# A two-layer graph network with experts on one core: the first six tiles of layer 1 begun in a branch beside layer 0's last blocks, and the last outputs added by pairs of tiles

## The chip, the core and the metric

The kernel runs on one core of a Trainium2 chip. A core has five engines, each with its own queue of instructions in a fixed order: PE (TensorE, matrix products), DVE (VectorE), ACT (ScalarE), POOL (GpSimd) and SP (SyncE, here only a sender of transfers). Transfers between the chip's memory (DRAM) and the core's on-chip memory are carried out by DMA engines, which all queues share. The metric is the device time of one execution in microseconds (us); the time of a kernel is the median of its runs.

## The reference, cut to what matters

```python
# layer 0
x = x + relu(adj @ (layernorm(x) @ W) + b)
x = x + moe(layernorm(x))        # 8 experts, the two best per row, hidden size 1024, relu
# layer 1
x = x + relu(top700(tanh(adj * adj) where adj > 0) @ (tanh(layernorm(x) @ W_proj + b_proj) @ W_gcn) + b_gcn)
x = x + moe2(layernorm(x))       # 8 experts, the two best per row, hidden size 256, gelu, plus its input
```

There are 3327 rows of 256 numbers in float32, and adj is 3327 x 3327, with about nine entries per row that are not zero. In both mixtures of experts each row goes to the two experts with the best scores, and the two results are added to it with weights.

## The kernel before, in words

Rows lie in 26 tiles of 128. `x` and `s` are on chip for all tiles: `x` holds the rows, `s` the features that the graph step multiplies by adj. Six large buffers, `ring[0]` to `ring[5]`, hold pieces of adj, weights of experts, or expert outputs that are read back, one after another.

Each layer goes through these stages:

1. *Features.* Every tile is normalized (`statistics` at L244 makes mean and inverse deviation, with two DVE instructions a tile and then twelve small ones for the whole group; `layernorm` at L266 writes `xn`), turned by PE (`by_features`, L278), and multiplied by one or two weight matrices (L288, L1019), which gives `s`.
2. *Aggregation* (`aggregate`, L321). For 13 panels of 256 columns of adj, PE forms the product with `s` (L335), and DVE adds bias, relu and x. After each panel the rows are normalized, scored and written to a list per expert in DRAM, `xlist`, by indirect transfers from POOL (L459).
3. *Expert blocks* (`experts`, L683). A block is up to 256 rows of one expert ("pair", 128 rows are a "single"). Its `step` (L830) has SP load list rows and weights of a later block into the ring (L734 to L756), PE turns rows (L767) and multiplies twice (L778 with ACT's function at L785, then L811), DVE adds the bias and scales (L818, L819), and POOL scatters the result rows to `ys` in DRAM (L459). The first eight blocks of a layer (EARLY) are planned from the first 18 tiles (`plan_early`), while the aggregation still runs; `plan` places the others. With these inputs layer 0 runs 30 blocks, numbered 0 to 29. Blocks 28 and 29 are pairs, 27 is a single. A branch (`rest`, L848) holds four spare singles, which are skipped here.
4. *Seam or end.* Both result rows of each row are read back from `ys` into the ring (`load_outputs`, L873, on SP's queue) and added to `x` by two DVE instructions (`add_loaded`, L884). Between the layers this is the head of layer 1's features: `turned_pairs` (L1001) goes through groups of tiles, first one of two, then six of four (FOURS, L82), alternating between `ring[5]` and `ring[4]`: read, add, statistics, normalize, turn. A read waits for all scatters of layer 0 (`follow`). At the end of the kernel `finish` (L1130) does read, add and output.

Layer 1's end already has a branch (L1136): if the first 14 tiles are complete after the early blocks, their results are read, added and written between the last blocks; the tiles from 14 on follow in `finish`. In the other arm all tiles follow. `covered` (L621) makes the flag on DVE, from the number of rows that the first tiles send to each expert and the number of rows that the early blocks do.

What sets the order: the program is written in the order of the source, and a planner of the compiler sorts the instructions of each stretch without branches onto the engines' queues, by its own model of when they are ready, the earlier in the source first; all waits are inserted by it. `issue_after` (in `behind`, L202) puts the instructions of a block behind a given one on that one's engine. It adds no wait between engines. Instructions inside a branch are not mixed with those outside. `declare_no_dep` and the groups next to it say which transfers need not wait for one another.

Of the kernel before, what the change touches and what calls it, by code (L numbers as in the profile page):

```python
# [10 lines left out]
F32 = mybir.dt.float32  # L11
BF16 = mybir.dt.bfloat16
I32 = mybir.dt.int32
AF = mybir.ActivationFunctionType
# [8 lines left out]
P = 128  # L23
# [53 lines left out]

FIRST_TILES = 14
FREE_PAN = NPAN - RING // NCHUNK
# [6 lines left out]
def gnn_moe_two_layers(  # L86
# [91 lines left out]

    ids_i = const.tile([P, NT, K], I32, name="ids_i")
    nc.gpsimd.iota(ids_i, pattern=[[K * P, NT], [1, K]], base=0, channel_multiplier=K)  # L180
    ids = const.tile([P, NT, K], F32, name="ids")
    nc.vector.tensor_copy(ids, ids_i)

    spare_i = const.tile([P, LATE, SG], I32, name="spare_i")
    nc.gpsimd.iota(spare_i, pattern=[[SB, LATE], [P, SG]], base=SPARE, channel_multiplier=1)
# [57 lines left out]

    def statistics(t0, n):  # L244


        st = work.tile([P, n, 6], F32, name="ln_st")
        mv = work.tile([P, n, 2], F32, name="ln_mv")
        for g in range(n):
            nc.vector.bn_stats(out=st[:, g, :], in_=x[:, t0 + g, :])  # L250
            nc.vector.bn_aggr(out=mv[:, g, :], in_=st[:, g, :])
        ve = work.tile([P, n], F32, name="ln_ve")
        nc.vector.tensor_scalar(ve, mv[:, :, 1], EPS, None, ALU.add)  # L253
        half = work.tile([P, n], I32, name="ln_half")
        nc.vector.tensor_scalar(half, ve.bitcast(I32), 1, None, ALU.logical_shift_right)
        guess = work.tile([P, n], I32, name="ln_guess")
        nc.vector.tensor_scalar(guess, half, -1.0, float(0x5F3759DF), ALU.mult, ALU.add)
        rs = guess.bitcast(F32)
        nw = work.tile([P, n], F32, name="ln_nw")
        for _ in range(3):  # L260
            nc.vector.scalar_tensor_tensor(nw, rs, -0.5, rs, ALU.mult, ALU.mult)  # L261
            nc.vector.tensor_tensor(nw, nw, ve, ALU.mult)  # L262
            nc.vector.scalar_tensor_tensor(rs, nw, 1.5, rs, ALU.add, ALU.mult)  # L263
        return mv, rs

    def layernorm(t0, n, stats=None, at=0):  # L266


        mv, rs = stats or statistics(t0, n)
        xn = work.tile([P, n, K, RW], F32, name="xn")  # L270
        for g in range(n):
            last_normalized[:] = [nc.vector.tensor_scalar(  # L272
                xn[:, g, 0, 0:D], x[:, t0 + g, :], mv[:, at + g, 0:1], rs[:, at + g : at + g + 1],
                ALU.subtract, ALU.mult,
            )]
        return xn
# [652 lines left out]
    def count(pan, chunks):  # L929
# [9 lines left out]
    layer0 = experts(  # L939
        p0, 3, xlist0, ys0, "0", FIXED[0], H, AF.Relu, f0_w1T, f0_b1, f0_w2T, f0_b2,  # L940
        nc.vector.tensor_copy,
# [49 lines left out]
    late = plan()  # L991
    layer0.rest(late, number_of_singles(late))
    rows_written.clear()

    first_pool.close()
# [5 lines left out]
    def turned_pairs():  # L1001


        for i, (t0, n0) in enumerate(FOURS):

            yt = ring[RING - 1 - i % NCHUNK][:, 0 : n0 * K * D]
            yt = yt.rearrange("p (n d) -> p n d", n=n0)
            with ExitStack() as queue:
                if normal:
                    queue.enter_context(tc.issue_after(normal[-1].ins))  # L1010
                add_outputs(yt, ys0, t0, n0)
                stats = statistics(t0, n0)
                for at in range(0, n0, 2):
                    xnT = by_features(layernorm(t0 + at, 2, stats, at), 2)
                    if at + 2 == n0:
                        normal.append(last_normalized[0])
                    yield t0 + at, xnT
# [118 lines left out]
    with tc.If(complete > 0) as arms:  # L1136
# [18 lines left out]
        layer1.rest(late, n_singles)  # L1155
        finish([(t, n) for t, n in FOURS if t >= FIRST_TILES])
    with arms.Else():
# [144 lines left out]
```

## Time and profile before

| what | value |
|---|---|
| median of 3 runs | 1272.45 us (1272.04 to 1273.16) |
| the profiled execution, its own time | 1283.92 us |
| its span, from the first to the last instruction | 1282.1 us |
| PE busy | 1208.2 us, 94% of the span |
| DVE, ACT, POOL busy | 713.0 (56%), 519.5 (41%), 286.3 us (22%) |
| chain: PE's aggregation, L335 | 23% of the span |
| chain: DVE's adding of expert outputs, L887 | 1% of the span |
| last scatter of layer 0 | sent at 747.40 us |
| last scatter of layer 1 | sent at 1260.45 us |

The profile page gives busy times by engine, then the chain of work that ended last, followed back from the last instruction, then groups of instructions by source line. The trace behind it answers closer questions: a timeline of single instructions, in which a bracket tells how long the engine was idle before and who released it, and tables of windows. A busy PE is not a PE at its peak, since its instructions overlap. In rows such as `L887 TENSOR_TENSOR x<-x,ring` the line is that of the source, and `out<-in` are the names of the tiles.

### The profile page before, as it was taken

The numbers are of one execution on the slowest core, as the hardware profiler recorded it, in microseconds if no ns is written. First come the engines' busy times: TensorE is split into PE (matmuls) and PEld (weight loads), VectorE is DVE, ScalarE is ACT, GpSimd is POOL, SyncE is SP. The second block draws the span as 40 slices with busy tenths as digits, with TensorE's granted clock in tenths as the row PEclk, the third lists the DMA queues.
The fourth block names the chain that finished last, engine by engine and source line by source line (L and its number), as shares of the span: only waits on it lengthen the run. The fifth ranks groups of instructions, "written<-read, shape, count | busy, mean of one in ns | idle before, by whom it ended". The sixth has DMA issues, their size and how long they took to land. (4 is left out here: it accounts for less than half of the span.)

```text
span 1282.1 us, 18560 instructions
## 1 busy us (share of the span) xinstructions
PE 1208.2 (94%) x5815; PEld 1036.9 (81%) x5815; DVE 713.0 (56%) x2918; ACT 519.5 (41%) x963; POOL 286.3 (22%) x364
## 2 busy tenths in 40 slices
PE   5999999999999999999999959999999999989991
PEld 4888888888888888888888847788888888867771
DVE  8167677676761111111111149579989998574453
ACT  3797545550122222322222215985554551133330
POOL 2132131221321111111111100203123131354432
PEclk9999999999999999999999979999999999999996
DMA  9676454453167566666666357145544452547785
GB/s 362 161 253 207 169 194 177 176 180 122 59 236 234 185 213 200 218 205 210 211 207 209 110 209 281 60 156 193 177 168 169 161 188 75 185 138 212 210 270 192
DMA packets 119458, 241.70 MB, mean 189 GB/s; under 512 B 21472, under 2 KB 89840, under 8 KB 112304
## 3 DMA queue, kind: packets, MB, share of 16 engines
q1 hardware_dynamic: 106576, 206.91, 48.7%
q0 software_dynamic: 11184, 31.85, 6.8%
q10 hardware_dynamic: 1584, 1.57, 0.4%
q8 instruction: 52, 0.85, 0.3%
q14 instruction: 62, 0.51, 0.1%
HBM read 203.99 MB, written 36.33 MB: 187 GB/s over the span
## 5 line engine op out<-in xcount | busy, mean ns | idle before, releaser
L335 PE MATMUL ps_g<-s,ring 128*128 128x256 f32 x2704 | 588.3, 380 | 1.6 <-issue 1.6
L335 PEld LDWEIGHTS ps_g<-s,ring 128*128 128x128 f32 x2704 | 511.9, 190 | 70.5 <-issue 1.7
L785 ACT ACTIVATE hT<-ps_h,ring 128x256 f32<-128x256 f32 (+1 forms) x304 | 139.1, 459 | 369.5 <-PE ps_h L778 322.1
L778 PE MATMUL ps_h<-xT,ring 128*128 128x256 f32 (+1 forms) x1208 | 259.9, 368 | 4.0 <-ACT xT L770 2.1
L778 PEld LDWEIGHTS ps_h<-xT,ring 128*128 128x128 f32 x1208 | 212.0, 191 | 43.4 <-ACT hT L785 4.8
L811 PE MATMUL ps_y<-ring,hT 128*128 128x256 f32 x928 | 208.7, 380 | 0.0
L355 DVE SCALAR_TENSOR_TENSOR rt_product<-xn,gate 128x256 f32<-128x256 f32 x400 | 197.6, 494 | 12.5
L459 POOL DMA_INDIRECT ys<-y,index x114 | 111.8, 981 | 408.2 <-DVE y L819 278.5
L811 PEld LDWEIGHTS ps_y<-ring,hT 128*128 128x128 f32 x928 | 173.5, 191 | 21.9
L459 POOL DMA_INDIRECT xlist<-xn,rt_idx x104 | 105.7, 1016 | 378.9 <-DVE ln_ve L253 288.4
L934 ACT ACTIVATE sign<-ring,below 128x416 bf16<-128x416 f32 x208 | 133.5, 642 | 74.4 <-DMA ring<-in_adjT 51.7
L818 DVE TENSOR_TENSOR y<-ps_y,ring 128x256 f32<-128x256 f32 x64 | 27.1, 424 | 154.8 <-PE ps_y L811 154.8
L770 DVE COPY xT<-ptb 128x512 f32<-128x512 f32 (+1 forms) x30 | 19.7, 655 | 161.5 <-PE ptb L767 161.5
L1046 ACT ACTIVATE ring<-ring 128x3328 f32<-128x3328 f32 x22 | 65.5, 2977 | 91.4 <-DVE ring L1045 57.8
L300 DVE TENSOR_TENSOR gnn_t<-ps_g,gnn_b_sb 128x256 f32<-128x256 f32 x52 | 22.0, 423 | 116.1 <-PE ps_g L335 116.0
L1047 ACT ACTIVATE ring<-ring 128x3328 f32<-128x3328 f32 x22 | 65.5, 2978 | 0.7
L811 PE MATMUL ps_y<-s,hT 128*128 x200 | 51.2, 395 | 10.8 <-issue 4.8
L811 PEld LDWEIGHTS ps_y<-s,hT 128*128 128x128 f32 x200 | 35.6, 191 | 20.4 <-issue 10.6
L420 ACT ACTIVATE rt_d<-rt_d 128x2 f32<-128x2 f32 x26 | 5.3, 202 | 114.1 <-DVE rt_d L419 114.1
L887 DVE TENSOR_TENSOR x<-x,ring 128x1024 f32<-128x1024 f32 (+1 forms) x34 | 33.0, 972 | 30.0 <-DMA ring<-ys 29.7
L250 DVE BATCH_NORM_STATS2 ln_st<-x 128x6 f32<-128x256 f32 x104 | 42.8, 420 | 4.8 <-DMA x<-in_x 3.7
L819 DVE TENSOR_SCALAR y<-y,ring 128x256 f32<-128x256 f32 x114 | 42.1, 371 | 3.6 <-DVEq L850 0.3
(171 smaller groups left out, 906.1 us busy)
## 6 DMA issues: line engine op xcount, KB each, us to landing
ring<-in_adjT SPq DMA_DIRECT2D x52, 1664.0 KB
ring<-in_f_w1T SPq DMA_DIRECT2D x30, 1024.0 KB
ring<-in_f_w2T SPq DMA_DIRECT2D x30, 1024.0 KB
ring<-xlist SPq DMA_DIRECT2D x52, 258.0 KB
ring<-ys SPq DMA_DIRECT2D x9, 1024.0 KB
ring<-in_f_w SPq DMA_DIRECT2D x36, 256.0 KB
ring<-in_f_b SPq DMA_DIRECT2D x34, 128.0 KB
xlist<-hT SPq DMA_DIRECT2D x16, 258.0 KB
```

The costliest lines, as they stand in the source:

```text
L250: nc.vector.bn_stats(out=st[:, g, :], in_=x[:, t0 + g, :])
L335: nc.tensor.matmul(ps[it], lhsT=chunks[k][:, c, ts(it, P)], rhs=s[:, j, :], start=(j == 0), stop=(j == NT - 1),)
L355: nc.vector.scalar_tensor_tensor(product, xn[:, g, 0, 0:D], 1.0, gate[:, e, :], ALU.mult, ALU.mult, accum_out=sc[:, g, e : e + 1],)
L459: d = nc.gpsimd.indirect_dma_start(out=a[:, :], out_offset=bass.IndirectOffsetOnAxis(ap=index, axis=0), in_=rows_, in_offset=None,)
L778: nc.tensor.matmul(ps, lhsT=w1[:, c, ts(hc, P)], rhs=xT[:, c, :], start=(c == 0), stop=(c == DC - 1),)
L785: nc.scalar.activation(hT[:, hc, :], ps, func, bias=bb1[:, hc : hc + 1])
L811: last_product[:] = [nc.tensor.matmul(ps, lhsT=hT[:, hc, ts(g, P)], rhs=w2[:, hc, :], start=(hc == 0), stop=(hc == hc_n - 1),)]
L819: last_y[:] = [nc.vector.tensor_scalar(y[:, g, :], y[:, g, :], xb[:, g, WT : WT + 1], None, ALU.mult)]
L887: nc.vector.tensor_tensor(x_t, x_t, yt[:, :, k * D : (k + 1) * D], ALU.add)
L934: nc.scalar.activation(sign, a[:, :, ts(i, GROUP)], AF.Sign, bias=below, accum_out=positive[:, pan, i, k : k + 1],)
L1046: nc.scalar.activation(a, a, AF.Square)
L1047: nc.scalar.activation(a, a, AF.Tanh)
```

## The change

Six tiles (BEGUN) are begun inside layer 0. After block 26 a flag is read: are all rows of the first six tiles done by the early blocks? If so, the last three blocks run in an arm that has more in it: after block 27 SP reads the outputs of tiles 0 and 1 and of tiles 2 to 5 into `s`, which is free then, and after block 28 DVE adds them to `x`, makes the statistics of all six tiles (kept in `begun_stats`) and normalizes tiles 0 and 1 (kept in `begun_xn`). If not, the other arm runs the same blocks and does this work after them. In `turned_pairs` the first group then has only the turning left, and the second group its normalizing; the first read of the seam is that of tiles 6 to 9. To make room, two integer tables share one buffer, and layer 0's `y` and `index` have two buffers instead of three. At the end, in the complete arm, tiles 14 to 25 are read, added and written by twos instead of by fours.

```diff
-FIRST_TILES = 14
+BEGUN, FIRST_TILES = 6, 14
...
-    ids_i = const.tile([P, NT, K], I32, name="ids_i")
+    ids_i = work.tile([P, NT, K], I32, name="wide_i", bufs=1)
...
-    spare_i = const.tile([P, LATE, SG], I32, name="spare_i")
+    spare_i = work.tile([P, LATE, SG], I32, name="wide_i", bufs=1)
...
-    def statistics(t0, n):
+    def statistics(t0, n, kept=None):
...
-        mv = work.tile([P, n, 2], F32, name="ln_mv")
+        mv, guess = kept or (
+            work.tile([P, n, 2], F32, name="ln_mv"), work.tile([P, n], I32, name="ln_guess")
+        )
...
-        guess = work.tile([P, n], I32, name="ln_guess")
...
-    def layernorm(t0, n, stats=None, at=0):
+    def layernorm(t0, n, stats=None, at=0, xn=None):
...
-        xn = work.tile([P, n, K, RW], F32, name="xn")
+        if xn is None:
+            xn = work.tile([P, n, K, RW], F32, name="xn")
...
     layer0 = experts(
-        p0, 3, xlist0, ys0, "0", FIXED[0], H, AF.Relu, f0_w1T, f0_b1, f0_w2T, f0_b2,
+        p0, 2, xlist0, ys0, "0", FIXED[0], H, AF.Relu, f0_w1T, f0_b1, f0_w2T, f0_b2,
         nc.vector.tensor_copy,
     )
...
     late = plan()
-    layer0.rest(late, number_of_singles(late))
+
+
+    flag = covered(BEGUN, late[4][:, 0:E])
+    n_singles = number_of_singles(late)
+    layer0.steps_to(late, EARLY)
+    written = list(outputs)
+    layer0.steps_to(late, layer0.always - 4)
+    layer0.step(late, name="xT_arms")
+    complete = nc.values_load(flag[0:1, 0:1], min_val=0, max_val=1)
+    before_branch = layer0.state()
+    begun_stats = (
+        const.tile([P, BEGUN, 2], F32, name="begun_mv"), const.tile([P, BEGUN], I32, name="begun_rs")
+    )
+    begun_xn = work.tile([P, 2, K, RW], F32, name="xn")
+    begun, in_s = [], s.rearrange("p n d -> p (n d)")
+    for t, n in FOURS:
+        if t < BEGUN:
+            yt = in_s[:, 0 : n * K * D] if not begun else in_s[:, 2 * K * D : (2 + n) * K * D]
+            begun.append((yt.rearrange("p (n d) -> p n d", n=n), t, n))
+
+    def begin():
+        for b in begun:
+            add_loaded(*b)
+        mv, rs = statistics(0, BEGUN, begun_stats)
+        layernorm(0, 2, (mv, rs), 0, begun_xn)
+
+    with tc.If(complete > 0) as arms:
+        layer0.step(late)
+        for yt, t, n in begun:
+            load_outputs(yt, ys0, t, n, written, "read0")
+        layer0.step(late)
+        with behind(last_y):
+            begin()
+        layer0.rest(late, n_singles)
+    first_arm = outputs[len(before_branch[3]) :]
+    with arms.Else():
+        layer0.back_to(before_branch)
+        layer0.rest(late, n_singles)
+        for yt, t, n in begun:
+            load_outputs(yt, ys0, t, n, outputs)
+        begin()
+    outputs.extend(first_arm)
     rows_written.clear()
...
-            with ExitStack() as queue:
-                if normal:
-                    queue.enter_context(tc.issue_after(normal[-1].ins))
-                add_outputs(yt, ys0, t0, n0)
-                stats = statistics(t0, n0)
+            with behind(normal):
+                if t0 < BEGUN:
+                    stats = begun_stats[0], begun_stats[1].bitcast(F32)
+                else:
+                    add_outputs(yt, ys0, t0, n0)
+                    stats = statistics(t0, n0)
                 for at in range(0, n0, 2):
-                    xnT = by_features(layernorm(t0 + at, 2, stats, at), 2)
+                    if t0 + at == 0:
+                        yield t0, by_features(begun_xn, 2)
+                        continue
+                    xn = layernorm(t0 + at, 2, stats, t0 + at if t0 < BEGUN else at)
+                    xnT = by_features(xn, 2)
...
-        finish([(t, n) for t, n in FOURS if t >= FIRST_TILES])
+        finish([(t, 2) for t in range(FIRST_TILES, NT, 2)])
```

## The prediction

> **What bounds the kernel now.** I read the page's chain first: the aggregations (PE, L335) and the expert blocks are PE's, and the change touches neither. So I went to the two stretches that it does touch, the seam between the layers and the end of the kernel. In the chain in order of time (start, us, what; whole lines, pieces under 0.4 us left out) the seam reads:
>
> ```profile
> 747.40 2.42 DMA ys<-y,index
> ...
> 750.51 3.60 DMA ring<-ys
> ...
> 754.12 0.70 DVE x L887
> ...
> 759.76 1.15 DVE x L887
> ```
>
> Layer 0's last output rows are scattered at 747.40, land at 749.82, SP sends the read of tiles 0 and 1 at 750.51, it lands 3.60 us later, and from then on every link is DVE's. PE has nothing from 746.27 (746.0 plus 0.27 busy in that slice) to 759.49. The timeline shows the period (start, us, engine, line):
>
> ```profile
> 767.73 2.48 DVE L887 TENSOR_TENSOR x<-x,ring 128x1024 f32<-128x1024 f32 x2
> 774.49 1.38 DVE L272 TENSOR_SCALAR xn<-x,ln_mv,ln_guess 128x256 f32<-128x256 f32 x4
> 775.78 2.48 DVE L887 TENSOR_TENSOR x<-x,ring 128x1024 f32<-128x1024 f32 x2
> ```
>
> A group of four tiles costs DVE 775.78 - 767.73 = 8.05 us, six times over. Windows of one period (length, then PE, PEld, DVE, ACT, POOL busy, clock, DMA share, GB/s) show who is close behind:
>
> ```profile
> 778.05:786.10 8.05, 7.34 (x38) 5.93 (x37) 7.46 (x27) 4.01 (x10) 0.00 (x0) 1.00 0.86 328
> 786.10:794.15 8.05, 7.61 (x40) 6.27 (x39) 7.46 (x27) 4.12 (x11) 0.00 (x0) 1.00 0.50 178
> ```
>
> DVE is full (7.46 busy, the rest about 0.02 us between its 27 instructions); PE needs 7.34 to 7.61 of 8.05, so it follows DVE but can make up only 0.4 to 0.7 us a group. ACT and DMA have room. Layer 1's aggregation begins at 819.02, 9.3 us after DVE's last normalized tile (809.76).
>
> The end of the kernel, from the timeline:
>
> ```profile
> 1260.45 0.97 POOL L459 DMA_INDIRECT ys<-y,index  x1 [2.80 <-DVE y L819]
> 1263.31 2.79 SPq L874 DMA_DIRECT2D ring<-ys  x3
> 1269.11 2.48 DVE L887 TENSOR_TENSOR x<-x,ring 128x1024 f32<-128x1024 f32 x2 [8.94 <-DMA ring<-ys]
> 1271.67 6.39 ACTq L1134 DMA_DIRECT2D out_x<-x  x3
> 1272.44 2.48 DVE L887 TENSOR_TENSOR x<-x,ring 128x1024 f32<-128x1024 f32 x2 [0.84 <-DMA ring<-ys]
> 1275.13 2.48 DVE L887 TENSOR_TENSOR x<-x,ring 128x1024 f32<-128x1024 f32 x2 [0.20 <-DMA ring<-ys]
> ```
>
> Three 1 MB reads land one after another, about 3.0 us apart; the adds of the last end at 1277.61 and its 0.5 MB of output takes the last 4.5 us.
>
> **The change, part by part.** *Seam.* Reads, adds and statistics of tiles 0 to 5, and the normalizing of 0 and 1, leave the seam. After it DVE's first group with a read behind it is tiles 6 to 9, whose adds begin at 767.73 now. Their read becomes SP's first, at 750.51 as now, since it waits for the same last scatter. A read of 512 KB took 3.60 us there; the first 1 MB read at the end took 1269.11 - 1263.31 = 5.80. I take 5.80, the row of its own shape; 754.11 (as fast as the small one) and 759.5 (one period of 3.2 us more, if a second read shares its way) are the ends. So the adds begin at 756.31 instead of 767.73: **-11.4** (ends -13.6 and -8.2). The normalizing of tiles 2 to 5 (four of 0.35 us) lies in DVE's wait before that. Everything after keeps its 8.05 us period.
>
> *What that work costs beside layer 0.* Two reads more on SP's queue behind the loads for the last block, sent by 714.86; SP is then idle to 750.51. Their 1.5 MB take about 4 us at the 390 GB/s of 754 to 756, in a stretch where the DMA share is 0.10 (720 to 740). DVE's part is queued between the last product of block 28 and the first of block 29, and behind it on DVE are block 29's index and y:
>
> ```profile
> 742.86 0.42 DVE L818 TENSOR_TENSOR y<-ps_y,ring 128x256 f32<-128x256 f32 x1 [9.30 <-PE ps_y L811]
> ```
>
> It is 1.42 + 2.48 (adds) + 2.6 (six tiles of statistics at the 1.75 us that a group of four takes) + 2.5 (twelve small operations, 0.2 apart) + 0.73 (two tiles normalized) = 9.7 us, against an idle of 9.30. The first y is 0.4 us to 0.8 us late, the second (746.31, 3.45 us later) is not, and that one carries the last scatter: 0. If the reads landed after about 736 each us would go on to the end; they have 18 us from their issue, and the longest such read in the trace takes 4.7 us (1242.95 to 1247.67).
>
> *The branch.* The flag is one small matmul and four short DVE operations in blocks where DVE works 2.5 us of 14; nothing. The flag will be set: from the inputs, tiles 0 to 5 send at most 214 rows to any expert, and each expert has its first 256 rows done among the eight early blocks. Layer 1 has the same branch, and the wait at it is:
>
> ```profile
> 1206.57 0.63 PE L767 MATMUL ptb<-ident,ring 128*128 128x128 f32 x4 [0.41 <-issue]
> ```
>
> The period of layer 1's blocks is no longer across it than elsewhere (single to pair 2.81 us there, 2.87 later). In layer 0 PE is the bound, so I pay the whole 0.41: **+0.4** (0 to 3.7, the largest stall of an engine without a visible cause in the trace).
>
> Leaving the arm, each engine jumps over the other arm, which is long on PE. The nearest row is the start of layer 1's aggregation, where PE passes the arm not taken:
>
> ```profile
> 822.25 7.93 PE L335 MATMUL ps_g<-s,ring 128*128 128x256 f32 x36 [1.55 <-issue]
> ```
>
> Two jumps (the spare singles, then the other arm) at 1.55: PE starts tiles 0 and 1 at about 749.4. Here a rule speaks against the change: the Trainium skill, page "TensorE: Matmul & The Clock Gate", section "Part 1: The HAM clock gate", says that the array falls to half clock after an idle window of about 3.4 us and needs as long to come back. The trace has the fall earlier:
>
> ```profile
> 746.00:748.00 2.00, 0.27 (x2) 0.00 (x0) 0.78 (x2) 0.00 (x0) 0.60 (x1) 1.00 0.00 0
> 748.00:750.00 2.00, 0.00 (x0) 0.00 (x0) 0.00 (x0) 0.00 (x0) 0.37 (x1) 0.60 0.20 70
> ```
>
> The clock column is 1.00, then 0.60, so it fell about 2.1 us into the idle time. By the rule PE would start warm at 749.4, and by the row cold. Cold costs what the first pair paid at 759.49: transposes 1.12 for 0.60, products 3.78 for 1.89, so 2.7 us with the features. A pair takes PE 3.75 us (half of 7.5), so three pairs end at 760.7 warm, and at 764.4 cold with 1 us until the first products flow. DVE's next tiles are ready at 756.31 + 6.76 = 763.1. By the rule no cost, by the row a lag of 1.3 us that PE makes up in three groups; I take **+0.2**. The other engines' jumps end before 756 as well.
>
> *Buffers.* y and index with two buffers instead of three: block t then waits for the scatter of block t-2, 2.4 us long, with blocks of 14.3 us (7.8 for a single): 0. The integer table shared at the start makes one POOL instruction wait for DVE's cast at 11.98; what may stand behind it is the load of proj_sb, sent at 3.58 and used at 14.34. If it is sent behind it, at 12.5, it lands 1 us late: 0 to 1.2, and I take **+0.2**, as the planner can put the load first.
>
> *End.* Six reads of 512 KB and six outputs of 256 KB. The reads still need 3.0 us a MB and outputs now begin among them, so the last lands at about 1275.3; two adds of 0.70 instead of two of 1.24, end at 1276.8; the last output is half as large, 3.4 us instead of 4.5 (its second 256 KB at the 236 to 258 GB/s of 1276 to 1280). End at 1280.2: **-1.9** (-3.5 if the writes fill the gaps, -0.3 if more requests slow the reads). SP sends six instead of three, 0.6 us each, ahead of the 1.5 us that each needs to land.
>
> *Code that moves.* ACT has two stalls of 3.73 and 3.05 us without a visible releaser, at 1149.46 and 1257.46, both on layer 1's path. If they hang on where code lies, they may go or double: 0, ends -3 and +3.7.
>
> Sum: -11.4 + 0.4 + 0.2 + 0.2 - 1.9 = -12.5. The profiled execution took 1283.92 us by its own time for a span of 1282.1, 0.9% above the median of 1272.45; I expect a span of 1269.6, an own time of 1271.4, and take the same 12.5 us off the median: **1260.0**.
>
> **Rivals.** *PE becomes the bound at the seam* (16%). If both jumps cost 3.7 us, PE starts at 753.7 cold, ends three pairs at 768.6, 5.5 us behind DVE, and makes up 0.55 a group in five groups: 2.7 us remain, and with a read that lands at 757.5 it is 1264. For it: PE is at 91 to 95% in the windows above. Against: both jumps at the largest stall.
>
> *The read lands early and the stall at 1257.46 goes as well* (6%): -13.6 instead of -11.4, and -3.05: 1254.8.
>
> *Adjacency pieces go ahead of the reads* (9%). Today SP sends piece by piece behind the reads (756.15, 762.70, 770.70, 778.70). With two reads gone the planner may put the four free pieces in front of the first read. A piece is 1.66 MB, 4.3 us at 390 GB/s. One or two in front: 1264 to 1269 (5%). All four, sent from 748: 17 us, so that the read lands at 771, 3.6 us later than the adds of tiles 6 to 9 begin now; with the end's -1.9 and the other +0.8 it is 1275, **slower** (4%). It decides from a landing at 768.8. Against: in the trace reads that were ready went first.
>
> *The flag is 0* (3%): the other arm does the same work after the blocks, DVE saves 2.5 us of small operations and waits about 3 longer for its first tile; with the end, 1271. The counts speak against it.
>
> **How the numbers follow.** My case 66%, at 1256.5 to 1263 with its unknown ends. Below 1269.9 or above 1275.0 counts as a change (0.2%, about what a measurement of this kernel can tell from none). Faster: 66 + 16 + 6 + 4 = 92%; same: 4% (the flag, and 1 of the pieces); slower: 4%. The range of 1256 to 1265.5 takes in my case but for a sliver at its ends, the first rival, and some of the pieces: about 8 in 10.
>
> **What would show it.** For the seam: adds of tiles 6 to 9 about 8.9 us after the last scatter (756.31 - 747.40), the period of 8.05 after them, and layer 1's aggregation 60 us after that scatter, where it is 71.6 us now (819.02 - 747.40). DVE's row between the last y of block 28 and the first of block 29 shows 9.7 us of work and no wait for a read. PE idle by over 0.7 us at the branch, or a PE that is no longer idle for xn by 800, would make me wrong on +0.4 and +0.2; For the end: six pairs of adds, the last done 16.3 us after the last scatter (17.2 now) and the span over 19.7 us after it (21.6 now). What would make the prediction wrong at large is another order of SP's queue.

## The result, and the profile after

The changed kernel takes 1264.89 us (median of 4 runs, 1262.91 to 1265.64), the kernel before 1272.6 beside it: ratio 0.9937, 95% interval 0.992 to 0.9954. That is 7.7 us faster (5.9 to 10.2); the forecast was 12.5. The time lies in the range, and the sign is right, but two terms of the sum are well off, one gain was not forecast, and without that gain the time would have been about 1266.7, outside the range of 1256 to 1265.5. That it lies inside is in part luck.

The profiled executions can't be set against each other whole: that of before took 1283.92 us, 11.3 over its median, and that of after 1264.53. A second profile of before, taken later, has an own time of 1276.9, and its seam agrees with the first within 0.1 us. So I compare stretches, each counted from layer 0's last scatter.

The seam after, from the timeline (start, us, engine, line; only these instructions):

```profile
743.54 0.97 POOL L461 DMA_INDIRECT ys<-y,index  x1 [2.48 <-DVEq L852]
...
746.00 1.97 PE L286 MATMUL pt<-ident,xn 128*128 128x128 f32 x8 [3.60 <-DVE xn L274]
746.78 1.71 SPq L876 DMA_DIRECT2D ring<-ys  x2
747.79 3.78 PE L1072 MATMUL ps_p<-xnT,proj_sb 128*128 128x256 f32 x8
748.71 0.57 SPq L319 DMA_DIRECT2D ring<-in_adjT  x1
752.96 2.49 DVE L889 TENSOR_TENSOR x<-x,ring 128x1024 f32<-128x1024 f32 x2 [7.40 <-DMA ring<-ys]
...
759.73 1.38 DVE L274 TENSOR_SCALAR xn<-x,ln_mv,ln_guess 128x256 f32<-128x256 f32 x4
760.28 0.67 PE L286 MATMUL pt<-ident,xn 128*128 128x128 f32 x4 [1.17 <-DVE xn L274]
...
761.02 1.22 DVE L889 TENSOR_TENSOR x<-x,ring 128x1024 f32<-128x1024 f32 x1
```

This is the forecast picture. The reads are SP's first instructions behind the scatter, ahead of the adjacency piece; the adds of tiles 6 to 9 begin 9.42 us after the scatter (8.9 forecast, 20.33 before); the period is 761.02 - 752.96 = 8.06; PE starts cold on the pair that was normalized early (3.78 us for products of 1.89) and is waiting for DVE again at 760.28. DVE's last normalized tile comes 51.46 us after the scatter, 62.36 before: -10.9.

The other end of the seam is not the forecast picture. PE at the start of layer 1's aggregation, after (timeline):

```profile
803.95 2.28 PE L294 MATMUL ps_s<-g_wg_sb,h2T 128*128 128x256 f32 x8
809.11 13.15 PE L337 MATMUL ps_g<-s,ring 128*128 128x256 f32 x52 [2.88 <-issue]
```

and the windows over it (length, PE, PEld, DVE, ACT, POOL busy, then the granted clock, DMA share, GB/s):

```profile
806.00:808.00 2.00, 0.23 (x2) 0.00 (x0) 0.00 (x0) 2.00 (x5) 0.00 (x0) 1.00 0.03 8
808.00:810.00 2.00, 0.89 (x4) 0.85 (x5) 0.00 (x0) 2.00 (x4) 0.00 (x0) 0.97 0.04 8
810.00:812.00 2.00, 2.00 (x6) 1.53 (x6) 0.00 (x0) 2.00 (x4) 0.00 (x0) 0.50 0.00 0
812.00:814.00 2.00, 2.00 (x8) 1.64 (x7) 0.00 (x0) 2.00 (x3) 0.00 (x0) 0.68 0.00 0
```

PE waits 2.88 us before the first product (1.55 after some products, in the row that the prediction quotes), and then runs at clock 0.50 to 0.68, where the same stretch of before stays at 1.00. By the clock column half clock lasts about 3.4 us (0.12 + 2.00 + 1.28), which costs PE half of that, 1.7. The last feature comes 11.23 us behind DVE's last normalized tile, where it was 9.42. So the aggregation begins 65.57 us after the scatter (60 forecast, 71.6 before) and ends 361.38 us after it, 6.1 sooner than in before (367.4 and 367.5 in its two profiles), not 10.9.

The end, after (timeline):

```profile
1241.04 0.97 POOL L461 DMA_INDIRECT ys<-y,index  x1 [0.30 <-issue]
1244.56 4.51 SPq L876 DMA_DIRECT2D ring<-ys  x6
1248.73 1.42 DVE L889 TENSOR_TENSOR x<-x,ring 128x512 f32<-128x512 f32 x2 [8.41 <-DMA ring<-ys]
1250.18 9.35 ACTq L1181 DMA_DIRECT2D out_x<-x  x6
...
1257.71 1.42 DVE L889 TENSOR_TENSOR x<-x,ring 128x512 f32<-128x512 f32 x2 [0.67 <-DMA ring<-ys]
```

The last adds are done at 1259.13, 18.1 us after the last scatter (16.3 forecast, 17.2 before), and the span ends 3.7 us later. The first output is sent at 1250.18, while reads are still landing.

### The profile page after: what moved, and what is told of

The parts are those of the page before. It is cut to its first block, busy times and chain, and to the rows that moved or that the text cites. A ratio compares the mean times of both kernels' runs of the same rounds, so it can differ in the third digit from the quotient of the medians.

```text
span 1262.8 us, 18597 instructions
## 1 busy us (share of the span) xinstructions
PE 1203.9 (95%) x5816; PEld 1035.4 (82%) x5816; DVE 711.2 (56%) x2916; ACT 520.0 (41%) x963; POOL 285.2 (23%) x364
## 5 line engine op out<-in xcount | busy, mean ns | idle before, releaser
L780 PE MATMUL ps_h<-xT,ring 128*128 128x256 f32 (+1 forms) x1176 | 253.1, 368 | 3.4 <-ACT xT L772 2.1
L780 PEld LDWEIGHTS ps_h<-xT,ring 128*128 128x128 f32 x1176 | 206.2, 190 | 41.5 <-ACT hT L787 4.5
L357 DVE SCALAR_TENSOR_TENSOR rt_product<-xn,gate 128x256 f32<-128x256 f32 x400 | 197.7, 494 | 12.5
L889 DVE TENSOR_TENSOR x<-x,ring 128x512 f32<-128x512 f32 (+1 forms) x36 | 30.2, 839 | 30.8 <-DMA ring<-ys 30.3
```

The costliest lines, as they stand in the source:

```text
L357: nc.vector.scalar_tensor_tensor(product, xn[:, g, 0, 0:D], 1.0, gate[:, e, :], ALU.mult, ALU.mult, accum_out=sc[:, g, e : e + 1],)
L780: nc.tensor.matmul(ps, lhsT=w1[:, c, ts(hc, P)], rhs=xT[:, c, :], start=(c == 0), stop=(c == DC - 1),)
L889: nc.vector.tensor_tensor(x_t, x_t, yt[:, :, k * D : (k + 1) * D], ALU.add)
```

## The experiments

All were run beside the kernel before, and each ratio is to that kernel on the same chip. The first four ran on one chip and the next four on another, where before takes 1272.5; the last four ran on two more chips, where it takes 1279.1 (tanh_last, padded, no_other_arm) and 1282.8 (both), so their times are read by the ratio alone. All intervals are 95% intervals.

The milestones, in us after layer 0's last scatter, from the timelines. "Feature" is PE's last feature product, counted from DVE's last normalized tile; "aggregation" is the end of layer 1's aggregation, counted from that feature.

| kernel | last normalized | feature | aggregation | sum | ratio (95%) |
|---|---|---|---|---|---|
| before | 62.36 | 9.42 | 295.62 | 367.40 | 1 |
| after | 51.46 | 11.23 | 298.69 | 361.38 | 0.9937 (0.992 to 0.9954) |
| before_again | 62.38 | 9.42 | 295.71 | 367.51 | 1.0 (0.9991 to 1.0008) |
| seam_only | 51.68 | 11.22 | 298.72 | 361.62 | 0.9945 (0.9933 to 0.9957) |
| end_only | 62.35 | 9.43 | 295.19 | 366.97 | 0.9992 (0.9984 to 1.0) |
| sum_first | 51.72 | 11.23 | 293.89 | 356.84 | 0.9979 (0.9971 to 0.9988) |
| wide_only | 62.60 | 9.42 | 295.28 | 367.30 | 0.9986 (0.9978 to 0.9994) |
| other_arm | 61.90 | 11.27 | 295.86 | 369.03 | 1.0007 (1.0001 to 1.0014) |
| begun2 | 58.82 | 11.22 | 298.61 | 368.65 | 1.0 (0.9992 to 1.0008) |
| lighter_filter | 50.30 | 12.80 | 298.99 | 362.09 | 0.9941 (0.9928 to 0.9954) |
| tanh_last | 49.16 | 10.74 | 298.60 | 358.50 | 0.9932 (0.992 to 0.9944) |
| padded | 68.90 | 15.37 | 299.97 | 384.24 | 1.0125 (1.0105 to 1.0145) |
| no_other_arm | 51.97 | 9.30 | 296.01 | 357.28 | 0.9913 (0.9901 to 0.9926) |
| both | 51.25 | 9.49 | 295.79 | 356.53 | 0.9901 (0.9886 to 0.9915) |

**The parts.** The kernel before once more (before_again, a comment line added), the change with the old end (seam_only), and before with the new end (end_only).

Seam_only, against after:

```diff
-        finish([(t, 2) for t in range(FIRST_TILES, NT, 2)])
+        finish([(t, n) for t, n in FOURS if t >= FIRST_TILES])
```

End_only, against before:

```diff
-        finish([(t, n) for t, n in FOURS if t >= FIRST_TILES])
+        finish([(t, 2) for t in range(FIRST_TILES, NT, 2)])
```

> The kernel before, unchanged, for a second profile. Theory A: about 12 us of the first profiled execution (own time 1283.92, median 1272.6) were its own and not the kernel's. Then this one, with an own time near 1272.5, starts layer 0's aggregation near 44.6 us (as after the change) instead of 47.2, sends layer 0's last scatter near 743.5 to 744.5 instead of 747.4, and takes about 136 to 138 us instead of 145.6 from the end of layer 1's aggregation to the last scatter; the seam (last scatter to the end of layer 1's aggregation) stays at 367.5 us. Rival B: those stretches are the same as in the first profile, and the change itself shortened them, so that it lost as much somewhere else.

> The change with the end by fours as before. Theory A (the end by pairs is worth nothing, since the reads now share the way with the outputs): 1264.9, within 0.7 us of the change, and 21.7 us from the last scatter to the end of the span. Rival B (the end by pairs costs, and hides a larger gain of the seam): 1263 or less. Rival C (it gains the forecast 1.9 us): 1266.8.

> The kernel before with only the end by pairs. Theory A: 1272.5, within 0.7 us. Rival B (it costs): 1274.5. Rival C (forecast): 1270.7.

Measured: 1272.38, 1265.57 and 1271.87 us (before 1272.51). By the medians the end by pairs is worth 0.6 to 0.7 us in either kernel; by its interval it is 0 to 2.0 in end_only, so it is hardly told from nothing. Nearly all of the gain is in the rest.

**The jump into the aggregation.** The branch that chooses between the top-k arm and the plain aggregation is turned round, so that the arm that is taken comes first and PE has nothing to pass before it.

```diff
-    with tc.If(most_reg > TOPK) as many:
-        with tc.tile_pool(name="topk", bufs=1) as tk:
...
-    with many.Else():
+    with tc.If(most_reg < TOPK + 1) as few:
+        aggregate(gnn_b_sb, filter_chunk, after1_but_last, loaded=ahead)
+    with few.Else():
...
-        aggregate(gnn_b_sb, filter_chunk, after1_but_last, loaded=ahead)
+        with tc.tile_pool(name="topk", bufs=1) as tk:
...
```

> The change with the two arms ahead of layer 1's aggregation exchanged: the aggregation lies directly behind the branch, the arm that is not taken behind it. Theory A (PE's wait of 2.88 us ahead of its first product, and half clock for 3 us after it, come from jumping over the other arm's code): the wait falls under 1 us and the clock stays at 1.00, 4 us earlier there; the jump then stands at the aggregation's end and costs 1.5 to 3 there; in all 1262 to 1263.5. Rival B (PE waits for data or for the register load): the wait stays at 2.9 and the time at 1264.9.

Measured: 1270.24. The aggregation begins at +62.78 with no wait and at full clock, and takes 294.06 us from its first product (295.8 with the jump): its end is 4.5 us earlier than in after. But the jump is not gone, it has moved behind the arm (sum_first, PE):

```profile
1101.07 0.17 PE L444 MATMUL pr<-cum,ones_sq 128*128 128x8 bf16 x1
1107.34 1.09 PE L769 MATMUL ptb<-ident,ring 128*128 128x128 f32 x4 [6.10 <-DMA s<-in_f_w]
```

PE stands for 6.10 us and runs at clock 0.50 after it. The bracket names a transfer of weights into `s`, but this turning does not read `s`, and in after the same instructions run at 1104.86 while the same transfer is under way (1100.64 to 1111.84). DVE stands 6.19 us at the same place, up to 1108.80, with no releaser. So the jump is the likelier cause; why it took twice as long here is open. From the end of the aggregation to layer 1's last scatter it takes 147.34 us, where after took 136.12. So 4.5 us were won and 11.2 lost.

**The start.** Only the shared integer table, in the kernel before.

```diff
-    ids_i = const.tile([P, NT, K], I32, name="ids_i")
+    ids_i = work.tile([P, NT, K], I32, name="wide_i", bufs=1)
...
-    spare_i = const.tile([P, LATE, SG], I32, name="spare_i")
+    spare_i = work.tile([P, LATE, SG], I32, name="wide_i", bufs=1)
```

> The kernel before, with nothing of the change but the shared integer table at the start. My theory: the 2.5 us by which layer 0's aggregation begins earlier in the changed kernel (44.6 to 45.4 us in three kernels that have the table, 47.2 to 47.9 in three that don't) come from this edit alone: POOL waits for DVE's cast, so its weight loads are sent at 10.6 to 13.1 us instead of 4.5 to 7.6 and no longer slow the small DVE operations in front of the first normalized tile. So the aggregation begins at 44.5 to 45.5 here, DVE's operations at 6 to 9 us take 0.15 each, and the time is about 1270.0 (ratio 0.998). Rival: the early start belongs to the smaller pool of the other edits (two buffers for y) or to chance, and then it begins at 47 to 48, 1272.5 us.

Measured: 1270.97, 1.8 us faster (0.8 to 2.8); layer 0's aggregation begins at 45.27 (47.20 and 47.87 in before). POOL in wide_only (timeline):

```profile
4.33 0.60 POOL L216 DMA_DIRECT2D gnn_b_sb<-in_g_b  x1
10.54 0.24 POOL L185 IOTA wide_i<- 128x52 int32 x1 [5.61 <-DVE slot L191]
10.75 0.58 POOL L216 DMA_DIRECT2D f_bg_sb<-in_f_bg  x1
```

and the same instruction of DVE in before and in wide_only:

```profile
7.66 1.08 DVE L257 TENSOR_SCALAR ln_guess<-ln_half 128x2 int32<-128x2 int32 x1
```

```profile
6.90 0.15 DVE L257 TENSOR_SCALAR ln_guess<-ln_half 128x2 int32<-128x2 int32 x1
```

POOL's wait for DVE's cast, which I had priced as a loss, holds back four weight loads and four memsets that in before run from 5.11 us on. Without them the small TENSOR_SCALAR operations of DVE on the way to the first tile take about 0.15 us instead of 0.64 to 1.08, and the first normalized tile begins at 9.26 instead of 10.95. What POOL does meanwhile in before:

```profile
6.88 0.75 POOL L211 DMA_DIRECT2D g_wg_sb<-in_g_wg  x1
...
7.67 1.05 POOL L915 MEMSET hT<- 128x516 f32 x2
```

The slow operation of DVE above ends at 8.74 and these memsets at 8.72; the two slow ones before it end at 6.95 and 7.63, where sends of POOL end at 6.93 and 7.63. So DVE was held until POOL's instruction was over, by sends and memsets alike.

**The branch and the dose.** In other_arm the flag is compared with 1, so that the late arm is always taken; the output is the same. In begun2 two tiles are begun instead of six.

```diff
-    with tc.If(complete > 0) as arms:
+    with tc.If(complete > 1) as arms:
```

```diff
-BEGUN, FIRST_TILES = 6, 14
+BEGUN, FIRST_TILES = 2, 14
```

> The changed kernel, with the flag compared with 1, so that layer 0's other arm is always taken: reads, adds and normalizing of the first six tiles come behind the last blocks, as before the change, but with the branch, the jumps, the shared table and the end by pairs. It computes the same. My theory: the branch by itself costs PE nothing that can be seen, so only the startup (-2.5) and the end (-0.7) remain of the gain: the aggregation of layer 1 begins 71 to 73 us after layer 0's last scatter, and the time is about 1269.3. Rival: the structure has a price of its own that the early work only covers (a jump into the arm, more code between blocks), and then layer 0's blocks take over 1 us longer than 404.9 us, or the seam is over 75 us, and the time is 1272 to 1275.

> The changed kernel with two tiles instead of six begun beside layer 0's last blocks. It computes the same. My theory: the seam is DVE's up to its last normalized tile, so with tiles 2 to 5 back behind the scatter one period of DVE is back, less what it spent waiting for the read: the last normalized tile comes 58 to 60 us after the last scatter (51.5 with six tiles, 62.4 before the change), the aggregation 71 to 73 less 2.0, that is 69 to 72 (65.6 and 71.6), and the time is 1268.5 to 1271. Rival: the gain of the seam is the read's place in SP's queue and not the number of tiles, and then two tiles give nearly all of it: under 1267.

Measured: 1273.2 and 1271.73, both slower than expected. The blocks cost nothing more (404.87 and 404.88 us from the aggregation to the last scatter, 404.78 in before_again), so no price lies there. In begun2 the last normalized tile is where I put it (58 to 60), but behind it the seam loses as much as in after, so that four tiles fewer leave no gain at all: the sum is 368.65, 1.1 over before's. With the first arm taken there is then the same loss behind it, with two tiles begun or with six. In other_arm half of it is there (feature 11.27) and half is not (aggregation 295.86). About 2 us of other_arm's time are not accounted for by its milestones, and stay open.

**ACT's filter.** ACT is busy without a gap at the end of the seam, since it filters the next panel of adj in quarters (square and tanh) between the features' operations. Lighter_filter lets DVE make the square, and puts DVE's first piece (1.9 us in after) behind the last normalized tile instead of ahead of the last group; tanh_last also queues ACT's part behind the last feature copy (`last_copy`, the only line shown here that lighter_filter lacks).

```diff
...
-        with tc.issue_after(normal[-2 if pan == 0 and k == 0 else -1].ins):
-            nc.vector.tensor_scalar(a, a, 0.0, None, ALU.max)
+        with tc.issue_after(normal[-1].ins):
+            nc.vector.scalar_tensor_tensor(a, a, 0.0, a, ALU.max, ALU.mult)
+        with tc.issue_after(last_copy[0].ins):
             for q in range(4):
                 part = a.rearrange("p c w -> p (c w)")[:, ts(q, PIECE // 4)]
-                nc.scalar.activation(part, part, AF.Square)
                 nc.scalar.activation(part, part, AF.Tanh)
```

> The changed kernel, with the filter of the adjacency panel that is made behind the seam rearranged: one operation of DVE does maximum and square (so that ACT has only the tanh, 16 operations of 0.9 us instead of 32), and its first piece goes behind DVE's last normalized tile instead of ahead of it. It computes the same. My theory: after the change the end of the seam is ACT's, which is busy without a gap from 800 to 810 us with these quarters between the features' own operations, and DVE carries a piece of 1.9 us ahead of the last group. So the last normalized tile comes 49.6 us after the last scatter (51.5), PE's last feature product 59 to 60 us after it (62.7), layer 1's aggregation 62 to 63.5 us (65.6), and the time is 1261.5 to 1262.5. Rival: PE's jump over the other arm and its fall to half clock set the start whatever comes before, or the DVE operation of two f32 inputs is slow enough (3.5 us instead of 1.9, four times) that the panel comes too late: no gain, 1264.5 to 1266.

> The lighter filter again (one DVE operation for maximum and square, only tanh on ACT), but with ACT's sixteen tanh operations queued behind the last feature copy, where the lighter filter still had them between the features' operations. It computes the same. My theory: the end of the seam is set by the order of ACT's queue, not by the amount of its work, which is why halving the work alone gained nothing. So PE's last feature product now comes 58 to 60 us after layer 0's last scatter (62.7 in the changed kernel, 63.1 with the lighter filter); the first quarters of tanh (0.9 us each) are done within PE's wait of about 3 us at the jump, so layer 1's aggregation begins 61.5 to 63.5 us after the scatter (65.6, 66.3), and the time is 1261 to 1262.5. Rival: the wait of PE before the aggregation is for the panel or for something else that ends at a fixed time, and the start stays at 65 to 66 us, 1265.

Measured: ratios 0.9941 and 0.9932. Halving ACT's work gains nothing: DVE's operation takes 3.62 us instead of 1.89, ACT waits 1.5 us for it once, with the features' operations queued behind, and the feature term grows to 12.80. Moving ACT's work behind the features shortens that term to 10.74, with PE busy without a gap. So the order of ACT's queue alone, at the same work, is worth 2.1 us. Against after the aggregation ends 2.9 us earlier, but only 0.5 of this is the feature term: DVE's last tile is normalized 2.3 us earlier, as DVE's piece has gone behind it and the first read's adds began 0.6 earlier. The ratio shows nothing of these 2.9 us beyond its interval: in the profile, layer 1's blocks of this kernel took 147.31 us on that chip.

**Where the jump costs.** Padded puts 64 products of one column in front of the seam's features, to shift PE's program; their result is thrown away.

```diff
+    pad = psh.tile([P, 1], F32, name="ps_p", tag="ph")
+    for _ in range(64):
+        nc.tensor.matmul(pad, lhsT=ident, rhs=ident[:, 0:1], start=True, stop=True)
```

> The changed kernel with 64 tiny products of PE (one column each, into a bank that nothing reads) at the start of the seam, where PE has nothing to do; they shift the place of everything behind them in PE's program. It computes the same and a little that is thrown away. My theory: the 2.88 us for which PE waits between the last feature and the first product of layer 1's aggregation is the fetching of code after the jump over the top-k arm, and what it takes depends on where the jump and its target lie in PE's program: it was 1.55 after some products in the kernel before, 1.66 after four products with the other arm taken, 2.79 and 3.17 ahead of the first product in two others. So the wait changes in size or place by over 0.5 us here, with the last feature still 62.5 to 63.5 us after the scatter: aggregation begun at 63 to 67, its end 359 to 364 (361.4), time 1262 to 1267. Rival: the wait hangs on when PE gets there, and stays at 2.8 to 2.9 us ahead of the first product: 1264.5 to 1265.5.

Measured: ratio 1.0125. I had taken the padding for nothing, and it is not (padded, PE; first the padding, then the aggregation's first products):

```profile
748.78 26.53 PE L1085 MATMUL ps_p<-ident 128*128 128x1 f32 x128
...
833.08 9.15 PE L337 MATMUL ps_g<-s,ring 128*128 128x256 f32 x29 [3.19 <-issue]
```

The 64 products appear as 128 and take 26.5 us, 0.21 each, nearly all of it at clock 0.50: the clock does not rise while they run. The wait stays ahead of the first product and at about 3 us (3.19), as the rival said. But the padding doesn't settle whether the place in PE's program counts. The page lists a DMA queue of kind "instruction" (packets, MB, share), in after and in padded:

```profile
q8 instruction: 54, 0.88, 0.3%
```

```profile
q8 instruction: 55, 0.90, 0.3%
```

A packet is 16 KB, and in the trace of before some 250 instructions of PE, weight loads included, lie between one packet and the next. The padding is 256 of them (128 products, 128 weight loads), so by this estimate it shifts the rest by one whole packet and leaves the place within a packet as it was. A shift by half a packet was not run.

**Without the branch.** No_other_arm always does the early work and leaves out the guard (the flag is 1 with these inputs); both adds the filter of tanh_last to it.

```diff
-    complete = nc.values_load(flag[0:1, 0:1], min_val=0, max_val=1)
...
-    with tc.If(complete > 0) as arms:
-        layer0.step(late)
+    layer0.step(late)
...
-    with arms.Else():
-        layer0.back_to(before_branch)
...
```

> The changed kernel without the branch of layer 0: the early reads, adds and normalizing are always done, without asking the flag (which is 1 for these inputs, so the output is the same). It leaves out the guard. My theory: the branch costs PE nothing beside the blocks and one late feature pair at most behind them, so layer 0's blocks take 404.8 us as before, the last normalized tile comes 51 to 52 us after the last scatter, and what differs is again the wait ahead of layer 1's aggregation: 1263 to 1265.5. Rival: the branch and the 1.8 us that ACT is later behind DVE's last tile in all kernels with it belong together; then the last feature comes 9.4 us behind the last normalized tile (11.2 with the branch), and the time is 1262 or less.

> The changed kernel without the branch of layer 0 (the guard is left out; the flag is 1 for these inputs) and with the tanh operations behind the last feature copy: the two versions that began layer 1's aggregation earliest, together. My theory: the two losses behind DVE's last normalized tile (ACT's order, PE's wait at the jump ahead of the first product) are then both small: last normalized tile 49 to 50.5 us after layer 0's last scatter, last feature 58 to 60 us, aggregation begun at 58 to 61 us and ended at 354.5 to 356.5 us after that scatter (361.4 in the changed kernel, 357.3 without the branch, 358.5 with the tanh behind), and the ratio to the kernel before is 0.988 to 0.991 (0.9937, 0.9913, 0.9932). Rival: the two are one and the same gain, since both only free PE from waiting in the same stretch; then the aggregation ends at 357 to 358.5 us and the ratio is 0.991 to 0.993.

Measured: ratios 0.9913 and 0.9901 (the first interval still overlaps that of after, by 0.0006). Without the branch the feature term is 9.30, as before the change, and the aggregation term 296.01: my theory that the branch costs nothing fell, and the rival's reading holds. PE there:

```profile
803.71 2.28 PE L294 MATMUL ps_s<-g_wg_sb,h2T 128*128 128x256 f32 x8
805.83 1.50 PE L337 MATMUL ps_g<-s,ring 128*128 128x256 f32 x6
809.14 13.22 PE L337 MATMUL ps_g<-s,ring 128*128 128x256 f32 x60 [1.82 <-issue]
```

Six products run first and the wait is 1.82, as in before. The version with both has the lowest ratio, and its interval lies below that of after. Beside no_other_arm its sum gains only 0.75 and the intervals overlap: its aggregation began at +62.00 and not by 61 as expected, since the first read's adds came 1.5 us later on that chip (10.89 against 9.42) and PE then waited 1.26 us for a filtered quarter. That the tanh helps once the branch is gone is not shown.

## Why the prediction was right in sign and too large

**The seam's reads, -11.4: right, -10.9.** The read took 752.96 - 746.78 = 6.18 us instead of 5.80, and was sent 3.24 us after the scatter instead of 3.11. These 0.5 us are all of the difference.

**The branch, +0.4: mis-sized, +4.8, and not where I looked.** Beside the blocks it is free: 404.88 us from aggregation to last scatter, 404.78 without it (406.05 in padded and 406.04 in no_other_arm, on one other chip). I asked what a jump delays at once, and PE passes it in time. The cost comes 60 us later, in two terms of the table. The feature term grows from 9.42 to 11.23 in every kernel with the branch that keeps the filter as it was, whichever arm runs (15.37 in padded, where PE itself comes late), and is 9.30 without it. ACT's queue shows how. Between the turning of the last two pairs before has one quarter of the filter (before):

```profile
809.64 0.59 ACT L285 COPY xnT<-pt 128x512 f32<-128x512 f32 x1 [0.48 <-PE pt L284]
810.13 0.90 ACT L1057 ACTIVATE ring<-ring 128x832 f32<-128x832 f32 x1
810.93 0.63 ACT L295 COPY s<-ps_s 128x256 f32<-128x256 f32 x2
811.45 0.61 ACT L285 COPY xnT<-pt 128x512 f32<-128x512 f32 x1
```

and after has two, and a feature operation (after):

```profile
795.44 0.58 ACT L287 COPY xnT<-pt 128x512 f32<-128x512 f32 x1
795.90 0.91 ACT L1104 ACTIVATE ring<-ring 128x832 f32<-128x832 f32 x1
796.70 0.47 ACT L1079 ACTIVATE h2T<-ps_p,g_bp_sb 128x256 f32<-128x256 f32 x1
797.06 0.91 ACT L1103 ACTIVATE ring<-ring 128x832 f32<-128x832 f32 x1
797.97 0.37 ACT L297 COPY s<-ps_s 128x256 f32<-128x256 f32 x1
798.23 0.59 ACT L287 COPY xnT<-pt 128x512 f32<-128x512 f32 x1
```

DVE's last tile is normalized at 809.76 and 795.00; its turned copy begins 1.69 us later in before and 3.23 in after (1.59 in no_other_arm, with no quarter between). The planner sorted the seam anew once the branch stood before it, and ACT's order came out 1.5 us worse for the last pair. No row of before could show the new order. What its timeline does show, and I passed over, is that ACT has one gap of 0.48 us between 804 and 821, so that whatever is put in front of a copy there delays it by its whole length.

The aggregation term grows from 295.6 to about 298.7 in after, seam_only, begun2, lighter_filter and tanh_last, and to 299.97 in padded. In all of these PE leaves layer 0's first arm by a jump and comes later to the jump ahead of the aggregation. (Sum_first has the first jump too, but no arm to pass ahead of the aggregation, and its term is 293.89.) In other_arm, whose program differs from after's in one constant, it is 295.86, with a wait of 1.66 after four products; without the branch it is 296.01. So what PE passes in layer 0 changes what the later jump costs.

The rows say more. PE goes on at nearly the same time in all thirteen profiles with that jump, 2.6 to 3.2 us after its last feature product: 822.25 - 819.18 = 3.07 in before, 809.11 - 806.23 = 2.88 in after, 809.14 - 805.99 = 3.15 in no_other_arm. What differs is how many products of the aggregation run before PE stops: seven in before, before_again, end_only and wide_only, four to six in other_arm, no_other_arm and both, none in the six above. In the kernel called both, 1.26 us of the time passes in a wait for a filtered quarter, and only 0.21 of waiting is left behind five products. So the jump itself did not get longer; PE had nothing at hand to do in it. The 3 us are the 1.3 us more of waiting and half clock behind it, 1.7.

How the earlier jump does this is open. The Trainium skill, page "Runtime: NRT & Kernel Launch", section "Instruction fetch mechanics", says that code is fetched ahead in order and that a jump out of the fetched part has to wait. That fits the trace of after, where between 806.2 and 809.2 us one packet moves on all DMA queues, and it is one of the instruction queue. Where the packets end after the first jump may decide how many products are at hand 60 us later, but no run here tests it. The largest stall that I allowed, 3.7 us, I put at the first jump, where PE had time for it; and it is not the largest in the trace of before, where ACT stands 8.20 us without a releaser before 389.17.

**PE's lag, +0.2: no cost seen.** The first pair did run cold; PE waited for DVE again at 760.28, within one group. The clock in after, around the seam's first product:

```profile
743.00:745.00 2.00, 0.00 (x0) 0.00 (x0) 1.23 (x4) 0.00 (x0) 0.97 (x1) 1.00 0.06 16
745.00:747.00 2.00, 1.00 (x5) 1.00 (x6) 0.56 (x2) 0.00 (x0) 0.00 (x0) 0.50 0.20 66
```

It fell at 745.0, 2.6 us after PE's last product (746.00 - 3.60 = 742.40), earlier than by the rule. The rule would have the start cold as well, though, since PE waited 3.60 us and not the 3.1 that I expected. The clock at the aggregation I didn't ask about, and the length of the wait alone would not have told: in after it fell about 809.9, when PE had been at work again for 0.8 us after a wait of 2.88, and in lighter_filter it stays at 1.00 through a wait of 2.88 us for DVE (up to 761.64).

**The start, +0.2: wrong sign, about -2.** The wait was there as forecast (POOL goes on at 10.40 us, behind DVE's casts), and the load of proj_sb was ahead of it, as I assumed. What I left out is what POOL's work does to others: sends and memsets that nobody needs yet had been holding up DVE's small operations on the path to the first tile.

**The end, -1.9: mis-sized, -0.6 to -0.7 by the medians.** Reads and outputs do share the way, and the reads pay for it. From their sending to the last adds it was 13.15 us (1257.71 - 1244.56), where three large reads took 11.82 (1275.13 - 1263.31). The smaller adds won 1.1 of that back, so only the last output is shorter, 3.7 instead of 4.5. From the last scatter to the end of the span it is 20.4 to 22.5 us in the ten profiles with pairs, 21.3 in the mean, and 21.2 to 23.3 in the four with fours, 22.1 in the mean: 0.8, with much scatter, and no profile at the 19.7 that I forecast. The prediction had this as the end of its range at -0.3, "if more requests slow the reads".

**Beside layer 0, 0: right.** DVE's row from 729.34 to 738.61 is 9.3 us of work without a wait for a read, and y of block 29 is taken 0.38 us after DVE was free (after):

```profile
729.34 3.56 DVE L889 TENSOR_TENSOR x<-x,s 128x512 f32<-128x512 f32 x4
...
738.99 0.42 DVE L820 TENSOR_TENSOR y<-ps_y,ring 128x256 f32<-128x256 f32 x1 [0.38 <-PE ps_y L813]
```

It fits with 0.38 us to spare, not 0.4 late. **Code that moves, 0**: ACT's stalls of 3 to 4 us in layer 1's blocks without a visible releaser are in the first profile of before, in tanh_last, padded and both, and in none of the other ten profiles, so they don't hang on this change.

The sum as measured: -10.9 at DVE, +1.8 and +3.0 behind it, -2 at the start, -0.6 at the end, that is -8.7, against -7.7 (-5.9 to -10.2) by the runs. The loss behind DVE and the unforecast gain at the start partly cancel, which is the luck in the total. The rivals: adjacency pieces did not go ahead of the reads (in its sum 771 is 3.3 us behind 767.73, not 3.6, which makes 1274.6), the flag was set, and PE was not the bound at the start of the seam. What was lost at the seam's other end, in ACT's order and in PE's jump, no rival named.

## What to carry to other kernels

When a stretch is shortened on the engine that bounds it, follow its last item through every later engine to the next stage, and price each wait there as well as the item's own start: here 4.8 of 10.9 us were lost between DVE's last tile and the next stage. A branch can be free where it stands and still cost later, by the order in which what follows is planned and by what PE waits for at its next jump; compare with a version without the guard before you call it free. And ask of every send and memset at the start who is held up meanwhile; doing later what is needed later was a gain by itself.

## What the runs showed of the hardware

- At the jump ahead of the aggregation PE went on 2.6 to 3.2 us after its last feature product, in thirteen profiles. The wait that shows was 1.1 to 1.8 us where four to seven products ran first, and 2.8 to 3.2 where none did, which was so in all six kernels in which PE had left an earlier arm by a jump. Turning the branch round moved the cost instead of removing it (PE stood 6.10 us behind the arm).
- The clock fell 2.1 and 2.6 us after PE's last product (before and after, at the seam); a wait of 2.88 us was followed by half clock in after and by full clock in lighter_filter.
- Small DVE operations (TENSOR_SCALAR, 128x2) took 0.64 to 1.08 us instead of about 0.15 while POOL sent weight loads and wrote memsets, and ended within 0.03 us of the end of a POOL instruction.
- Products of one column in float32, 64 in the source and 128 in the trace, took 0.21 us each, and the clock stayed at 0.50 under them: tiny products are no free filler.
- DVE's maximum of a 128x3328 float32 tile took 1.89 us, maximum and product in one operation 3.62.
- The kernel before took 1272.5 us on two chips, 1279.1 on a third and 1282.8 on a fourth; layer 0's blocks took 404.8 to 404.9 us on the first two and 406.04 to 407.01 on the others. In the first profile of before they took 406.15, like those.
